# A third buffer for the second feed-forward weights, two small fp4 tiles fewer, and the planner's due times set anew

## The chip, the cores and the metric

The kernel runs on one core of one Trainium2 chip, as one program. The metric is the device time of one execution in microseconds; the time of a kernel is the median of several runs. TensorE (PE) does the matrix products and its share of the transposes, VectorE (DVE), ScalarE (ACT) and GpSimd (POOL) work on tiles in SBUF, and all transfers are issued by SyncE (SP), whose queue is in order.

## What is computed

The input has 8 sequences of 1024 rows with 256 columns. Four blocks follow each other, each added to its input after a plain layer norm of it:

```python
x = x + L0_attn(layernorm(x))   # linear "flow" attention, 16 heads of 16, cumulative sums along the
                                # sequence; Wo; layer norm; gelu(h @ W1 + b1) @ W2 + b2, 256 -> 1024 -> 256;
                                # layer norm
x = x + L0_ffn(layernorm(x))    # relu(x @ w1 + b1) @ w2 + b2, 256 -> 1024 -> 256
x = x + L1_attn(layernorm(x))   # softmax attention, one head of 256, over the whole sequence
x = x + L1_ffn(layernorm(x))    # fp4: silu(q(x) @ q(wg).T) * (q(x) @ q(wu).T), then q(h) @ q(wd).T, 256 -> 704 -> 256
# q: blocks of 16, scale = max|x| / 6, each element rounded to the fp4 grid and multiplied by the scale
```

All of it is in float32.

## The kernel before, in words

The rows are cut into 64 chunks of 128, and four chunks make a group: `flows` is 16 groups, two for each sequence. Each part of the work is a Python generator: `linear_group`, `linear_span` and `linear_chunk` for the linear attention, `dense` for both feed-forward networks of 1024, `norms_1` and `norms_2` behind each of these, `soft_chunk` for softmax attention and the fp4 network, `fp4_weights` and `softmax_weights` for their weights. A generator yields what it needs next: an engine, the tiles that must be done, how many PSUM banks, and a due time `at`, counted in groups.

**The planner.** `Plan.run` chooses which generator goes on. It keeps a model time for each engine (`Plan.took` holds the costs), takes the part that can start soonest on PE's model clock, and among parts that could start now the one with the smallest due time. The order in which instructions are issued is pinned on all five engines, so the choices are made when the program is built, and on the chip each engine follows its list. The due times come from the table `T`; `EARLY` holds other values for stretches of PE's model time (until 130, 260, 400 and 2150 us), and where a name isn't in the stretch's own table, `T` holds. `weights` is the due time of the weight loads, `prods`, `sums`, `weighted`, `scores`, `chunk`, `xo`, `turn_h`, `turn_k` of steps of the linear attention, `soft`, `soft1` and the like of the softmax chunks; names with a number at the end (`lin1`, `weights0`) are added for that group alone. `ripe_*` says how long before PE needs it a part of each engine counts as ripe.

**Turning tiles.** `flip` transposes a tile of 128x256 in one of two ways. By DMA: POOL splits the floats into halves of 16 bits (`cut`), SP issues a DMA transpose (`spun`), ACT joins them again. On PE: two matmuls with the identity, and one copy by ACT. It takes PE where `plan.idle(1, times["ahead"])` finds that no other part would be ready for PE within `ahead` microseconds of the model, and in the first group.

**Filling.** Where the planner sees PE wait for more than 1.6 us, `fill` issues matmuls of the identity up to a little before the time at which the next part is expected.

**Weights of the dense networks.** They are not kept in SBUF: `load_weights` inside `dense` loads them again for each group, 256 KB at a time, two blocks `f` in one tile. `w_in` is the first matrix of each network, `w_out` the second; each has two buffers, and one tile serves both halves of a group through repeated loads. The rule for a load is

```python
at=p + 0.9 + due("weights", p) + (2 * n % 32 + (0 if first else LAG)) / 32,
when=lambda: n < bufs + used[0] // 2 and count["stage"] >= 2,
unused=ws[n - bufs :][:1] if n >= bufs else (),
```

with `bufs` from `W_IN` or `W_OUT`: load `n` may be issued when the tile `bufs` loads before it has been used up. `half` is a turned half of a group's activations, the moving operand of the products with `w_in`; `hidden` is the result after gelu or relu, and `second` multiplies it with `w_out`.

**fp4.** `fp4` quantizes a tile in place: `x_amax` (block maxima), `x_s` (scales), `x_r` (their reciprocals), then four passes of DVE and one of ACT. The scale tiles are small tiles in rotation, `x_s` of four buffers and `x_r` of three.

All engines' instructions carry line 417 in the profile, the line that issues them in `Queue`; so groups are told apart by the tiles' names.

Of the kernel before, what the change touches and what calls it, by code (L numbers as in the profile page):

```python
# [17 lines left out]
P = 128  # L18
# [5 lines left out]
INTER = 704  # L24
V_PADS = 2
HB = P // 2
SCW = P + HB
W_IN, W_OUT = 2, 2
RES = 10
HALVES = 5  # L30
T = dict(
    span=-0.073, prods=0.129, pair=0.137, sums=0.037, weighted=0.239, sums2=0.231, chunk=0.625,
    scores=0.819, turn_k=0.829, xo=0.419, turn_h=0.635, step=0.092, dense=-0.115, norm=0.522,
    soft=3.5, soft1=0.277, soft2=0.575, soft3=0.75, fp4=2.397, fp4_over=4.836, tail=11,
    weights=0.209, shy=0.745, ripe_t=1.247, ripe_v=0.744, ripe_s=0.298, ripe_g=0.0, ripe_d=6.94,
    back=0.511, ahead=0.946, stage=3, lin=0.0, lin0=0.01, lin1=0.0, lin2=0.0, lin3=0.0,
    dense0=0.0, dense1=-0.033, norm0=0.0, norm1=0.0, weights0=-0.412, weights1=0.023, gate0=0,
    gate1=1, by_act=1,
)
LAG = 2  # L40
QB = 16
# [35 lines left out]

EARLY = [
    (130.0, dict(
        prods=0.359, pair=0.052, weighted=0.011, sums2=0.405, scores=0.861, turn_k=0.81,  # L80
        xo=0.296, step=0.131, dense=0.051, soft=2.551, soft1=0.323, soft2=0.706, fp4_over=5.754,
        weights=0.044, ripe_t=1.058, ripe_v=0.456, ripe_s=0.249, ripe_g=0.541, ripe_d=9.276,
        lin3=0.344, dense1=-0.003, weights0=-1.017, weights1=0.043,
    )),
    (260.0, dict(
        span=-0.064, prods=0.185, sums=-0.114, chunk=0.702, scores=0.785, dense=-0.085,
        soft=3.213, soft1=0.121, weights=-0.008, ripe_s=0.838, back=0.505, lin=-0.259,
        lin0=-0.325, norm0=-0.157, norm1=-0.26, weights0=-0.379, weights1=0.063, gate1=3.5,
    )),
    (400.0, dict(  # L90
        prods=-0.044, turn_k=0.82, turn_h=0.707, step=0.103, norm=0.746, soft=3.784, soft3=0.912,
        fp4=2.195, weights=0.078, ripe_d=7.2, ahead=0.839, lin2=-0.414,
    )),
    (2150.0, dict(
        chunk=0.596, xo=0.47, norm0=-0.113, pair=0.211, sums=0.071, turn_h=0.706, dense0=-0.017,
        ripe_d=6.945, ahead=0.541, weighted=0.176, lin3=-0.528, soft3=1.013, prods=0.106,
        gate1=3, fp4=3.733, lin1=0.497, dense1=0.151, turn_k=0.801, weights=0.169, lin2=-0.186,
    )),
]

# [18 lines left out]
class Plan:  # L119
# [206 lines left out]
    def dve(self, *tiles, **kw):  # L326
        return self.need("vector", tiles, **kw)

    def act(self, *tiles, **kw):
        return self.need("scalar", tiles, **kw)  # L330
# [39 lines left out]
    def run(self):  # L370
        while self.parts:
            now = self.free.get("tensor", 0.0)
            best = None
            for part in self.parts:
                t = self.ready(part[1])
                if t is None:
                    continue
                stays = self.tiled and part[1].tiled
                queue = part[1].queue
                wait = max(max(t) - now - (0.3 if stays or part[2] < 0.0 else 0.0), 0.0)  # L380
                urgent = part[2] < 0.0
                unripe = 0.0 if urgent else max(t[1] + self.times[RIPE[queue]] - now, 0.0)
                key = wait, unripe, queue == "tensor", not stays, part[2]
                if best is None or key < best[0]:
                    best = key, part, max(t)
            assert best is not None, "every part waits for another"
            until = max(now, best[2])
            if until - self.ran > 1.6 and best[1][1].queue == "tensor" and self.fill is not None:
                if (self.banks_free(best[1][1].banks + 1) or 0.0) <= self.ran + 0.4:
                    self.fill(until - 0.6)  # L390
                    self.ran = until - 0.6
            if best[0][0] > 0.0 or best[1][1].queue == "tensor":
                self.free["tensor"] = max(now, best[2])
            part = best[1]
            need = next(part[0], None)
            if need is None:
                self.parts.remove(part)
            else:
                part[1] = need
                if need.at is not None:  # L400
                    part[2] = need.at
# [34 lines left out]
def block_stack_kernel(ctx: ExitStack, tc: tile.TileContext, a: dict, out: bass.AP):  # L436
# [50 lines left out]
    def fresh(kind, need, name=None):  # L487

        need.fresh = kind
        yield need  # L490
        return make(kind, name)
# [16 lines left out]
    def small(shape, name, bufs=4):  # L508
        t = sm.tile(shape, F32, tag=name, name=name, bufs=bufs)
        return t  # L510
# [275 lines left out]
    def blocks(t, width):  # L786
        return t[:, :width].rearrange("p (b e) -> p b e", e=QB)

    def wide(v, rows, nb):
        return v.unsqueeze(2).to_broadcast([rows, nb, QB])  # L790

    def fp4(src, width, rows=P, factor=1.0):

        nb = width // QB
        src = src[:rows, :width]
        amax = small([P, INTER // QB], "x_amax", 2)[:rows, :nb]
        nc.vector.tensor_reduce(
            amax, blocks(src, width), AX.X, ALU.max, apply_absolute_value=True
        )
        sc = small([P, INTER // QB], "x_s", 4)[:rows, :nb]
        nc.vector.tensor_scalar(sc, amax, factor / 6.0, 1e-12, ALU.mult, ALU.max)
        rc = small([P, INTER // QB], "x_r", 3)[:rows, :nb]
        nc.vector.reciprocal(rc, sc)  # L810
        yield dve(rc)
        nc.vector.scalar_tensor_tensor(
            blocks(src, width),
            blocks(src, width),
            -factor * (1.0 - 2.0**-23),
            wide(rc, rows, nb),
            ALU.mult,
            ALU.mult,
        )
        tile_c = yield from fresh("q_c", act(src))  # L820
        c = tile_c[:rows, :width]
        nc.scalar.activation(c, src, AF.Square, scale=(2.0**22 / 6.0) ** 0.5)
        yield dve(c)
        k = 2.0**22 * 4.0 / 3.0
        nc.vector.scalar_tensor_tensor(src, c, k, src, ALU.add, ALU.add)
        yield dve(src)
        nc.vector.scalar_tensor_tensor(src, c, k, src, ALU.add, ALU.subtract)
        plan.drop(tile_c)
        nc.vector.tensor_tensor(
            blocks(src, width), blocks(src, width), wide(sc, rows, nb), ALU.mult  # L830
        )

    def fp4_weights():
# [15 lines left out]
        for i, (src, turns) in enumerate(pieces):  # L849
            for j in range(i, min(i + 3, len(pieces))):  # L850
                if j not in raws:
                    ahead = pieces[j][0]
                    raws[j] = (yield from fresh(
                        "soft",
                        dma(at=times["fp4"] + times["fp4_over"] * i / len(pieces), when=lambda: count["stage"] >= times["stage"]),
                        "w_raw",
                    ))[
                        : ahead.shape[0], : ahead.shape[1]
                    ]
                    nc.sync.dma_start(out=raws[j], in_=ahead)  # L860
            rows, width = src.shape
            raw = raws.pop(i)
            at = times["fp4"] + times["fp4_over"] * i / len(pieces)
            yield dve(raw, at=at)
            yield from fp4(raw, width, rows)
            yield pe(raw, banks=1)
            bank = tr_bank()
            for k, (dst, c0, n) in enumerate(turns):
                nc.tensor.transpose(bank[:n, k, :rows], raw[:, c0 : c0 + n], ident[:rows, :rows])
            plan.drop(raw)  # L870
            yield act(bank)
            for k, (dst, c0, n) in enumerate(turns):
                nc.scalar.copy(dst, bank[:n, k, :rows])
# [55 lines left out]
    weights = set()  # L929
# [753 lines left out]
    def soft_chunk(cc):  # L1683
# [81 lines left out]
        n = yield from layernorm("soft", rows)  # L1765
        yield dve(n)
        yield from fp4(n, D)
        xqT = two((yield from fresh("soft", plan.pool(n, at=at + times["soft2"]), "xqT")))
        yield from flip(two(n), xqT, last=n)
# [26 lines left out]
        plan.drop(xqT)  # L1796
        yield dve(hid)
        yield from fp4(hid, INTER, factor=0.5)
        hqT, pairs = [], []
        for half in range(2):  # L1800
# [92 lines left out]
```

## Time and profile before

| | |
|---|---|
| median of three runs | 2453.99 us (2453.81 to 2455.13) |
| the profiled execution | 2454.87 us, span 2453.2 us |
| PE busy | 2423.9 us, 99% of the span, 16475 matmuls |
| DVE, ACT, POOL busy | 1915.0, 1390.8, 1276.8 us |
| mean granted clock of PE | 0.997 |
| w_out and w_in loads | 256 each, of 256 KB |
| DMA transposes | 770 |

The profile is of one execution. Times are in microseconds unless marked ns. PE is the matmuls, PEld the loads of the stationary operand beside them, SPq SyncE's queue. A row of a group reads: line, engine, operation, output<-inputs by tile names, shape, count; then busy time and mean of one in ns; then the idle time of the engine just before them and what ended it. A row of a stretch reads: its limits, its length, then for each engine the busy time and the number of instructions, then PE's granted clock, the busy share of the DMA engines and GB/s. A row of the order of time reads: start, duration, engine, line, operation, with the idle time before it and what ended that in brackets. `bank<-ident` with no other input is a filler; `bank<-ident,x` turns tile x on PE.

### The profile page before, as it was taken

How to read it: one execution, taken by the hardware profiler on the slowest of the kernel's cores; microseconds unless marked ns; L12 is line 12 of the kernel's file. 1: busy time of each engine (PE TensorE's matmuls, PEld its weight loads, DVE VectorE, ACT ScalarE, POOL GpSimd, SP SyncE). 2: the span in 40 equal slices, each digit the busy share in tenths (PEclk: the TensorE clock that was granted, in tenths of full speed). 3: DMA queues.
4: the chain of work that ended last, by engine and by line, in shares of the span. 5: the costliest groups of instructions: out<-in, count | busy, mean ns of one | idle time of the engine just before them, and what ended most of it. 6: DMA issues, size and time to landing. Idle time of an engine off the chain costs nothing.

```text
span 2453.2 us, 47660 instructions
## 1 busy us (share of the span) xinstructions
PE 2423.9 (99%) x16475; PEld 1893.4 (77%) x16475; DVE 1915.0 (78%) x4149; ACT 1390.8 (57%) x2901; POOL 1276.8 (52%) x2260
## 2 busy tenths in 40 slices
PE   8999999999999999999999999999999999999998
PEld 6878777777777777777777777787777777877766
DVE  7778787878779787787877887688786977755877
ACT  5454556565565645556565565655556565555563
POOL 4354556565555656365563655546455574544342
PEclk9999999999999999999999999999999999999999
DMA  3255455564655555546555555555555555545342
GB/s 106 82 158 159 123 153 127 138 145 121 145 136 123 136 140 129 139 114 155 132 121 134 127 151 127 132 133 129 139 129 130 138 124 140 126 130 124 71 85 54
DMA packets 631985, 313.00 MB, mean 128 GB/s; under 512 B 435392, under 2 KB 620224, under 8 KB 631744
## 3 DMA queue, kind: packets, MB, share of 16 engines
q1 hardware_dynamic: 631744, 309.96, 51.1%
q8 instruction: 130, 2.13, 0.4%
q14 instruction: 111, 0.91, 0.1%
HBM read 188.17 MB, written 20.71 MB: 85 GB/s over the span
## 4 chain that ended last, share of the span: by engine, by line
PE 85%; DVE 8%; POOL 2%; DMA 2%; issue 1%; ACT 1%; SPq 0%; DVEq 0%; POOLq 0%; ACTq 0%
PE bank L417 85%; DMA spun<-cut 2%; DVE hid L417 1%; DVE prod L417 1%; POOL cut L417 1%; DVE n L417 1%; DVE ln_st L417 1%; POOL ln_rstd L417 1%; DVE x_amax L417 0%; DVE sc L417 0%; DVE mx L417 0%; DVE q L417 0%; DVE u L417 0%; DVE k L417 0%; POOL ln_shift L417 0%
## 5 line engine op out<-in xcount | busy, mean ns | idle before, releaser
L417 PE MATMUL bank<-half,w_in 128*128 128x256 f32 x2048 | 530.1, 382 | 8.5 <-ACT half L417 7.2
L417 PE MATMUL bank<-w_out,hidden 128*128 128x256 f32 x2048 | 526.2, 384 | 0.9 <-DMA w_out<-in_L_attn_W_dram 0.8
L417 PEld LDWEIGHTS bank<-w_out,hidden 128*128 128x128 f32 x2048 | 378.1, 190 | 103.6 <-issue 45.7
L417 PEld LDWEIGHTS bank<-half,w_in 128*128 128x128 f32 x2048 | 385.2, 190 | 87.8 <-issue 22.7
L417 POOL TENSOR_SCALAR ln_ve<-ln_mv 128x1 f32<-128x1 f32 x384 | 107.4, 280 | 544.0 <-DVE ln_mv L417 525.0
L417 POOL TENSOR_TENSOR ln_rstd<-ln_ve,neghalf 128x1 f32<-128x1 f32 x384 | 250.4, 652 | 32.0
L417 ACT ACTIVATE hidden<-bank,c_L_ffn_b 128x256 f32<-128x256 f32 x256 | 120.7, 472 | 226.6 <-PE bank L417 225.1
L417 PE MATMUL bank<-n2T,qT 128*128 128x512 f32 x512 | 241.4, 594 | 0.1
L417 PE MATMUL bank<-vt,probT 128*128 128x256 f32 x1024 | 231.6, 379 | 0.0
L417 PEld LDWEIGHTS bank<-vt,probT 128*128 128x128 f32 x1024 | 194.1, 190 | 32.1 <-issue 6.0
L417 POOL COPY cut<-n 128x512 uint16<-128x512 uint16 x233 | 175.6, 759 | 80.9 <-DVE n L417 67.4
L417 ACT ACTIVATE hidden<-bank,c_L_attn_b 128x256 f32<-128x256 f32 x256 | 119.7, 469 | 172.0 <-PE bank L417 171.2
L417 POOL COPY cut<-prob 128x512 uint16<-128x512 uint16 x215 | 147.6, 708 | 88.5 <-ACT prob L417 51.9
L417 POOL COPY cut<-hid 128x512 uint16<-128x512 uint16 x169 | 114.4, 694 | 148.6 <-DVE hid L417 51.1
L417 PE MATMUL bank<-wdT,hqT 128*128 128x256 f32 x768 | 176.2, 379 | 0.0
L417 PE MATMUL bank<-wgT,xqT 128*128 128x352 f32 x512 | 173.8, 462 | 1.2 <-ACT xqT L417 1.2
L417 PE MATMUL bank<-wuT,xqT 128*128 128x352 f32 x512 | 172.4, 459 | 0.0
L417 ACT COPY probT<-spun 128x512 uint16<-128x512 uint16 x254 | 162.0, 674 | 12.7 <-DMA spun<-cut 12.3
L417 ACT ACT_TABLE_LOAD x126 | 161.7, 1283 | 4.4 <-PE bank L417 2.1
L417 PEld LDWEIGHTS bank<-wdT,hqT 128*128 128x128 f32 x768 | 145.4, 190 | 23.0 <-issue 1.2
L417 PEld LDWEIGHTS bank<-n2T,qT 128*128 128x128 f32 x512 | 96.3, 190 | 70.5 <-issue 56.4
L417 PEld LDWEIGHTS bank<-wuT,xqT 128*128 128x128 f32 x512 | 97.3, 190 | 54.2
(272 smaller groups left out, 4838.2 us busy)
## 6 DMA issues: line engine op xcount, KB each, us to landing
w_in<-in_L_attn_W_dram SPq DMA_DIRECT2D x128, 256.0 KB
w_out<-in_L_attn_W_dram SPq DMA_DIRECT2D x128, 256.0 KB
w_in<-in_L_ffn_w_dram SPq DMA_DIRECT2D x128, 256.0 KB
w_out<-in_L_ffn_w_dram SPq DMA_DIRECT2D x128, 256.0 KB
spread<-packed SPq DMA_DIRECT2D x90, 256.0 KB
spun<-cut SPq DMA_TRANSPOSE x770
x<-in_L_attn_inputs_dram SPq DMA_DIRECT2D x64, 128.0 KB
xr<-in_L_attn_inputs_dram SPq DMA_DIRECT2D x64, 128.0 KB
```

The lines of the kernel that those rows point to most:

```text
L417: ins = method(*args, **kw)
```

## The change

`W_OUT` goes from 2 to 3: a third buffer for the second matrix, 2 KB more in each partition. `x_s` goes from four buffers to three and `x_r` from three to two. The tables of `EARLY` get other values in all stretches, and a fifth table holds from 2150 on, where `T` alone held before. `fill` stops 1.0 us before the expected time and no longer 0.6.

```diff
-W_IN, W_OUT = 2, 2
+W_IN, W_OUT = 2, 3
...
 EARLY = [
     (130.0, dict(
-        prods=0.359, pair=0.052, weighted=0.011, sums2=0.405, scores=0.861, turn_k=0.81,
-        xo=0.296, step=0.131, dense=0.051, soft=2.551, soft1=0.323, soft2=0.706, fp4_over=5.754,
-        weights=0.044, ripe_t=1.058, ripe_v=0.456, ripe_s=0.249, ripe_g=0.541, ripe_d=9.276,
-        lin3=0.344, dense1=-0.003, weights0=-1.017, weights1=0.043,
+        prods=0.359, pair=0.052, weighted=0.011, sums2=0.405, chunk=0.557, scores=0.861,
+        turn_k=0.81, xo=0.296, turn_h=0.656, step=0.131, dense=0.051, soft=2.551, soft1=0.323,
+        soft2=0.706, fp4_over=5.754, weights=0.08, ripe_t=1.058, ripe_v=0.456, ripe_s=0.249,
+        ripe_g=0.541, ripe_d=9.276, lin3=0.344, dense1=-0.003, weights0=-1.017, weights1=0.043,
     )),
     (260.0, dict(
-        span=-0.064, prods=0.185, sums=-0.114, chunk=0.702, scores=0.785, dense=-0.085,
-        soft=3.213, soft1=0.121, weights=-0.008, ripe_s=0.838, back=0.505, lin=-0.259,
-        lin0=-0.325, norm0=-0.157, norm1=-0.26, weights0=-0.379, weights1=0.063, gate1=3.5,
+        span=-0.064, prods=0.34, sums=-0.114, weighted=0.339, chunk=0.702, scores=0.945,
+        dense=-0.085, soft=3.213, soft1=0.121, weights=-0.008, ripe_s=0.794, back=0.505,
+        lin=-0.259, lin0=-0.325, lin2=-0.983, dense1=-0.028, norm0=-0.157, norm1=-0.26,
+        weights0=-0.379, weights1=0.063, gate1=3.5,
     )),
     (400.0, dict(
-        prods=-0.044, turn_k=0.82, turn_h=0.707, step=0.103, norm=0.746, soft=3.784, soft3=0.912,
-        fp4=2.195, weights=0.078, ripe_d=7.2, ahead=0.839, lin2=-0.414,
+        span=-0.031, prods=-0.044, sums=0.149, scores=0.9, turn_k=0.82, step=0.103, norm=0.746,
+        soft=3.876, soft2=0.578, soft3=0.912, fp4=2.195, fp4_over=4.172, weights=0.238,
+        ripe_d=7.2, ahead=0.839, lin=0.187, lin2=-0.414, turn_h=0.816,
     )),
     (2150.0, dict(
-        chunk=0.596, xo=0.47, norm0=-0.113, pair=0.211, sums=0.071, turn_h=0.706, dense0=-0.017,
-        ripe_d=6.945, ahead=0.541, weighted=0.176, lin3=-0.528, soft3=1.013, prods=0.106,
-        gate1=3, fp4=3.733, lin1=0.497, dense1=0.151, turn_k=0.801, weights=0.169, lin2=-0.186,
+        prods=0.036, pair=0.211, sums=0.071, weighted=0.176, chunk=0.596, turn_k=0.801, xo=0.47,
+        turn_h=0.596, soft3=1.013, fp4=3.733, fp4_over=6.383, weights=0.104, ripe_d=6.945,
+        ahead=1.487, lin1=0.497, lin2=-0.186, lin3=-0.528, dense0=-0.017, dense1=0.151,
+        norm0=-0.113, norm1=0.103, weights0=-0.286, gate1=3,
+    )),
+    (1000000000.0, dict(
+        lin3=0.54, ripe_d=5.647, lin1=0.423, dense1=-0.052, scores=0.51, xo=0.287, chunk=0.609,
+        shy=0.81, back=0.523, sums2=0.353, weights0=-0.388, soft1=0.394, step=0.139,
+        ripe_v=1.456, ripe_s=0.503, ahead=1.562, lin=-0.002,
     )),
 ]
...
                 if (self.banks_free(best[1][1].banks + 1) or 0.0) <= self.ran + 0.4:
-                    self.fill(until - 0.6)
-                    self.ran = until - 0.6
+                    self.fill(until - 1.0)
+                    self.ran = until - 1.0
...
-        sc = small([P, INTER // QB], "x_s", 4)[:rows, :nb]
+        sc = small([P, INTER // QB], "x_s", 3)[:rows, :nb]
...
-        rc = small([P, INTER // QB], "x_r", 3)[:rows, :nb]
+        rc = small([P, INTER // QB], "x_r", 2)[:rows, :nb]
```

## The prediction

> **What bounds the kernel now.** I read the page first: busy times (part 1), and the slices (part 2).
>
> ```profile
> span 2453.2 us, 47660 instructions
> PE 2423.9 (99%) x16475; PEld 1893.4 (77%) x16475; DVE 1915.0 (78%) x4149; ACT 1390.8 (57%) x2901; POOL 1276.8 (52%) x2260
> PE   8999999999999999999999999999999999999998
> ```
>
> TensorE (PE) bounds it: it stands still for 2453.2 - 2423.9 = 29.3 us. A better order of the same work can win only that, the filler matmuls of the identity that the planner puts into expected gaps (the second row below, from the groups by form: 36.6 us), and matmuls run at the lower clock. All else on PE is in both kernels. So I asked where these three lie. First PE in stretches of the plan:
>
> ```profile
> L417 PE MATMUL bank<-w_out,hidden 128*128 128x256 f32 x2048 | 526.2, 384 | 0.9 <-DMA w_out<-in_L_attn_W_dram 0.8
> L417 PE MATMUL bank<-ident 128*128 128x128 f32 x288 | 36.6, 286 | 3.1 <-POOL ident masks.py:199 3.1
> 0.00:130.00 130.00, 117.87 (x1053) 95.65 (x1054) 98.28 (x234) 62.98 (x164) 48.28 (x102) 0.96 0.34 99
> 130.00:260.00 130.00, 125.45 (x1098) 102.38 (x1097) 105.19 (x254) 67.00 (x162) 66.56 (x128) 0.99 0.54 149
> 994.00:1288.00 294.00, 293.24 (x1999) 229.07 (x1998) 234.40 (x498) 170.57 (x350) 162.88 (x283) 1.00 0.54 133
> 2400.00:2453.20 53.20, 45.79 (x224) 35.34 (x222) 40.03 (x72) 19.47 (x37) 12.09 (x15) 1.00 0.21 50
> ```
>
> The second column is PE's busy time. Idle: 12.1 us before 130, 4.6 us from there to 260, 7.4 us after 2400, 0.76 us in a period of 294 us (two groups) of the steady part. Filler: 29.2 us (226 of 288) before 400, the other 7.4 us after 2400. From 260 to 2400 little is to be had: the waits of PE say 4.7 us on `half` (the six seams where the next group's turned activations arrive), and 0.3 us else.
>
> The one wait on `w_out` stands in the order of time at 208 us, just behind one on `w_in`:
>
> ```profile
> 202.90 1.89 PE L417 MATMUL bank<-half,w_in 128*128 128x256 f32 x8
> 206.11 1.13 PE L417 MATMUL bank<-half,w_in 128*128 128x256 f32 x4 [1.31 <-DMA w_in<-in_L_attn_W_dram]
> 208.02 1.78 PE L417 MATMUL bank<-w_out,hidden 128*128 128x256 f32 x4 [0.78 <-DMA w_out<-in_L_attn_W_dram]
> 209.59 1.91 PE L417 MATMUL bank<-half,w_in 128*128 128x256 f32 x4
> 211.30 1.24 PE L417 MATMUL bank<-w_out,hidden 128*128 128x256 f32 x4
> 212.37 1.72 PE L417 MATMUL bank<-ident 128*128 128x128 f32 x14
> 214.15 1.13 PE L417 MATMUL bank<-half,w_in 128*128 128x256 f32 x4
> ```
>
> Both weights come late, matmuls then run slow, and a filler stands before the next. The windows around it show the clock (busy time, then the granted clock after the bracket):
>
> ```profile
> 204.89:208.30 3.41, 1.41 (x5) 1.00 0.98 299
> 208.30:211.71 3.41, 3.41 (x9) 0.50 1.05 270
> 243.90:247.30 3.40, 1.84 (x60) 1.00 0.96 166
> 247.30:250.70 3.40, 3.38 (x61) 1.00 0.21 43
> ```
>
> A stretch of 3.41 us with 1.41 us of work was followed by 3.41 us at 0.50; one with 1.84 us was not. The other two drops of this trace follow stretches with 1.53 us (13.74 to 17.15) and 1.00 us (30.80 to 34.22).
>
> **The change part by part.** All sums are on the profiled execution: 2454.87 us, its span 2453.2 plus 1.7 around it; the median of the runs is 2453.99, so I take 0.9 us off at the end.
>
> 1. *Third `w_out` buffer.* No byte and no instruction is added: the 256 loads stay, each issued up to one tile earlier. Its direct price now is all the idle time before 2048 matmuls: 0.9 us, 0.78 of it at 208. Its indirect worth is in SP's order: a `w_out` load waits in SP for PE to release a buffer, and transposes, spreads and `w_in` queue behind it. At 202.97 `w_in` was issued, at 205.22 four `spread` loads, and the DMA engines were at 0.98 of their time (299 GB/s) when PE starved. With `w_out` already there, `w_in` and `w_out` needn't both be fetched in that burst. The stall costs 1.31 + 0.78 idle, 1.55 of half clock (12 matmuls from 208.02 to 212.16 in 4.14 us, at 0.216 each 2.59), and 1.78 of filler until 214.15: 5.4 us. Gone wholly: -5.4; moved elsewhere: 0. `w_in` keeps two buffers and is the first of the two late, so I take -4.0.
>
> 2. *Small scale tiles, 4 to 3 and 3 to 2.* Written by DVE and read by DVE in order; the trace shows no idle time before any `x_s` or `x_r` instruction. Nothing, hidden by DVE's own order. If a third quantization had to wait for a tile, one final multiply (892 ns) would be moved forward: up to +0.9 at a place, on an engine that is 78% busy. 0.
>
> 3. *Fill up to 1.0 us instead of 0.6 before the expected time.* Thirteen blocks of filler, each some 0.4 us shorter (5.2 us in all). This wins only where the filler still ran when the awaited tile was there. By the order of time: n was ready at 13.63 and turned at 13.94; `n0T` at 17.04, used 17.98; h at 66.76, turned 67.14; h at 101.67, turned 103.13; k long before 59.39; `hqT` at 2444.24, used 2444.71. Six blocks at most 0.4 each: -2.3. Against it: a longer gap can cost a clock drop, 3.41 / 2 = 1.7 us. The only gap that now follows a mid-run block is 0.53 (at 109.84), so 0.93 after the change, well short of the emptiness of the stretches that dropped. I take -1.5, bounds -2.3 to +1.7.
>
> The Trainium skill has a rule that bears on this: "TensorE: Matmul & The Clock Gate", Part 1, "What's actually happening", puts the half clock after at least one idle window of about 3.4 us. Taken as a wholly idle window, no gap of this kernel would cost clock and the longer margin would be free (-2.3); the rows above disagree, since a window 41% busy was followed by 0.50.
>
> 4. *Due times before 260.* They move DVE's and SP's order. Two waits stand out: the filler from 101.34 to 109.31, about 8 us while DVE finishes two h between scans, and 241.62 to 247.32, 1.88 of filler and 1.52 idle before `half`. In the new numbers the first stretch has chunk and turn_h of its own, the second later prods, weighted and scores, so other DVE work stands behind the layer norms. Both gone: -11.4. But DVE was busy 76% there (98.28 of 130), the two h still need 2.3 us of normalizing each, and new gaps open for the closed ones: bounds -6 to +5; I take -2.5.
>
> 5. *Due times of 260 to 2150, with `ahead` 0.541 to 1.487.* Five seams at 0.76 and one at 0.93 are 4.7 us. `ahead` asks whether PE has other work within that time; a larger one turns fewer tiles on PE and more by POOL, SP and DMA. From 400 to 2150 PE turns 34 blocks of n, k and h, 0.108 us each: 3.7 us, of which at most all is won. A turn by DMA takes a cut (0.7 us on POOL), a transpose (1.2 us on SP) and a copy (0.67 instead of 0.37 on ACT), and half of that path is what the seam waits on. Bounds -6 (both) to +8 (1.0 us more at each of eight seams); I take -2.5, as PE's own work is what bounds this part.
>
> 6. *A last stretch after 2150.* To 2400 PE is busy 249.94 of 250, so nothing. After 2400 there are 7.4 us idle and 7.4 us of filler, but that part follows DVE's chain of fp4 steps (0.8 to 0.9 us each on the chain of waits), which the change doesn't shorten; larger `ahead` takes the short way away there. -4 to +4; I take -1.0.
>
> 7. *What the third buffer adds.* Earlier `w_out` loads stand before transposes in SP's queue: 0.42 us of issue each, 256 KB in the DMA engines. Seen once per group in 16 groups, a tenth of it at a seam that shows: +0.5; and for gaps that open at new places I add +2.0, about the size of the largest wait now (1.9).
>
> Sum: -4.0 - 1.5 - 2.5 - 2.5 - 1.0 + 0.5 + 2.0 = -9.0. 2454.87 - 9.0 = 2445.9 profiled, 2445.0 for the median.
>
> **The rivals.** *No difference* (2449 to 2459): PE is 99% busy, the idle time on w_out is 0.9 us, and for each gap closed one of like size opens. For it: the steady part, 1750 us long, has almost nothing to give; against: before 130 alone there are 12.1 us idle and eight blocks with 196 of the 288 fillers (about 25 us), which one new order in the right direction cuts. I would put it at 2452, the certain -1.5 of step 3 and 0.5 from step 1. That the third buffer isn't used at all, because a due time and not a free buffer starts each load, belongs here for step 1 and leaves the rest: 2449.
>
> *Slower*: the load that is pulled forward meets the seam. In each of 16 groups PE waits at the seam for `half`, that is for the last transposes in SP's queue. If one `w_out` load is issued before them, they start 0.42 us later and share the DMA engines with 256 KB: the `w_in` load of 202.97 took until 206.1, 3.1 us. Priced at 1.0 us a group: +16, less 6 us of the gains at the start: 2454 + 10 = 2464. It decides as soon as a seam of the steady part shows over 1.0 us where it now shows 0.76 in two groups; past about 1.9 us of idle in 3.41 each would cost 1.7 us of clock besides. For it: 70.6 us in which POOL's cuts wait for transposes; against: the due time still orders the load, and `half` waits for a transpose that was itself late because of its cut.
>
> **How the numbers follow.** Faster as worked out: 0.66, 2445.0; its own range, by the bounds of steps 1, 3, 4, 5, 6 of which not all fall one way, 2431 to 2449. No difference: 0.13. Slower: 0.21, of which about half above 2462. The range 2431 to 2463 leaves out some 0.08 below and 0.10 above. 0.2% of the time, 4.9 us, is about what a measurement of this kernel can tell from no change; the chances for more, within and less than that are those of the three cases.
>
> **What would show it.** Right: no wait of PE on `w_in` or `w_out` near 205 and no half clock after 41 us; PE idle before 260 below 14 us (now 16.7) and filler in all below 32 us; the period of the steady part still 293 to 294 us, a span near 2444. Step 1 is wrong if PE waits there on `w_in` alone; step 3 if the clock drops more than three times after the first; step 5 if the seam gaps add up to over 6 us or the period grows; step 6 if the idle time after 2400 grows. Wrong as a whole: PE idle plus filler at or above 66 us, or a period above 295 us.

## The result: slower by 0.19%, and the profile after

The changed kernel takes 2459.79 us (median, 2457.36 to 2461.92), the kernel before on the same chip 2454.71 us (2452.63 to 2457.15): a ratio of 1.0019, 95% interval 1.0013 to 1.0026. The forecast was 2445.0. The profiled execution was the quickest of the changed kernel's runs, 2457.36 us with a span of 2455.3; so the trace shows 2.1 us of the loss (2455.3 - 2453.2), and the rest lies in its other runs, of which no trace is at hand. The mean granted clock of the sixteen was 0.9968, 0.998 in this one.

The page of the changed kernel: busy times, then from the groups by form the second matrix' products, the filler, and the layer norm output turned on PE; then four windows as before (limits, length, busy time of PE, PEld, DVE, ACT and POOL, clock, DMA share, GB/s).

```profile
span 2455.3 us, 47506 instructions
PE 2422.2 (99%) x16449; PEld 1887.9 (77%) x16449; DVE 1903.0 (78%) x4148; ACT 1393.5 (57%) x2906; POOL 1247.7 (51%) x2245
L425 PE MATMUL bank<-w_out,hidden 128*128 128x256 f32 x2048 | 523.1, 384 | 1.0 <-ACT hidden L425 0.9
L425 PE MATMUL bank<-ident 128*128 128x128 f32 x232 | 29.7, 286 | 3.1 <-POOL ident masks.py:199 3.1
L425 PE MATMUL bank<-ident,n 128*128 128x128 f32 x66 | 13.3, 292 | 5.2 <-ACT n L425 3.2 <-DVE n L425 1.9
0.00:130.00 130.00, 116.46 (x1029) 93.61 (x1030) 98.98 (x236) 63.45 (x165) 47.44 (x103) 0.97 0.37 103
130.00:260.00 130.00, 124.73 (x1089) 101.83 (x1087) 104.16 (x247) 62.53 (x157) 59.75 (x114) 0.99 0.53 151
994.00:1288.00 294.00, 293.49 (x2001) 228.21 (x2000) 233.02 (x494) 166.97 (x349) 159.55 (x279) 1.00 0.55 132
2400.00:2455.30 55.30, 49.19 (x229) 38.26 (x227) 42.34 (x83) 22.57 (x42) 13.65 (x21) 1.00 0.29 62
```

PE is busy 1.7 us less than before and idle 33.1 us instead of 29.3. The filler fell by 6.9 us, as it should; but before 260 PE is idle 18.8 us, not 16.7, and it turns more tiles itself (`n` 66 times instead of 46). The waits on the load of `w_out` are gone. The stall at 208 isn't:

```profile
205.96 1.03 PE L425 MATMUL bank<-w_out,hidden 128*128 128x256 f32 x4
210.12 1.87 PE L425 MATMUL bank<-half,w_in 128*128 128x256 f32 x4 [3.13 <-DMA w_in<-in_L_attn_W_dram]
211.78 1.91 PE L425 MATMUL bank<-w_out,hidden 128*128 128x256 f32 x4
213.49 1.14 PE L425 MATMUL bank<-half,w_in 128*128 128x256 f32 x4
```

That is PE in order of time. PE now starves once, 3.13 us on `w_in` alone, where it starved 1.31 on `w_in` and 0.78 on `w_out`. SP's queue in order of time says why:

```profile
201.06 2.50 SPq L425 DMA_DIRECT2D spread<-packed  x4
203.61 0.60 SPq L425 DMA_DIRECT2D w_out<-in_L_attn_W_dram  x1
204.25 0.47 SPq L425 DMA_DIRECT2D w_raw<-in_L_ffn_w_down_dram  x1
204.82 1.70 SPq L425 DMA_DIRECT2D w_in<-in_L_attn_W_dram  x2
```

The two loads of `w_in` are issued at 204.82, behind four `spread` loads, a `w_out` load and one of fp4 weights. The DMA engines were full meanwhile (1.00 of their time from 206.9 to 210.3; that window is shown at the end). The tile of the first of the two was last read by PE at 203.53 (the end of the matmuls of the load two before it), 1.3 us before its issue. So with two tiles the turn in the queue can hold at most 1.3 of the 3.13 us. The load then took 5.3 us from its issue to its use, where the one issued at 202.97 in the kernel before took 3.1; how much of that is the full DMA engines was not tested alone.

*Where the time went.* To see where in the run it was won and lost, I took from both traces the time at which PE had done the same useful matmuls: each counted at its usual distance from the next, fillers and turns on PE left out. The difference, after minus before, at eight times of the kernel before:

```
time in before (us)    121    248    295    406   1163   2336   2387    end
after                 -0.9   -6.8   +1.3   +1.0   -0.3   +6.7   +6.1   +1.9
```

So the start did win 6.8 us by 248. It lost 8.1 in the next 47 us (2.9 of gaps, 1.8 of filler, 1.1 of turns on PE, 2.3 of small delays), held until 1163, lost 7.0 in the second half of the steady part, and won 4.2 at the end. The total of +1.9 is made of -6.3 filler, -1.7 half clock, +3.2 turns on PE, +3.6 gaps, and +3.0 of delays between matmuls too small to be listed as idle time. A turn or a filler counts here at its usual distance, some 0.11 us; if the delay behind each turn is counted to the turn, the turns are +5.4 and the small delays +1.0.

The loss behind 248, PE in order of time in the changed kernel:

```profile
265.89 1.13 PE L425 MATMUL bank<-w_out,hidden 128*128 128x256 f32 x4
266.86 1.95 PE L425 MATMUL bank<-ident 128*128 128x128 f32 x16
...
274.58 0.41 PE L425 MATMUL bank<-ident,w_raw 128*128 128x128 f32 x2 [1.47 <-DVE w_raw L425]
274.99 2.86 PE L425 MATMUL bank<-half,w_in 128*128 128x256 f32 x12
...
279.14 1.13 PE L425 MATMUL bank<-w_out,hidden 128*128 128x256 f32 x4 [0.86 <-ACT hidden L425]
```

and in the kernel before:

```profile
272.37 1.99 PE L417 MATMUL bank<-w_out,hidden 128*128 128x256 f32 x8
274.20 1.03 PE L417 MATMUL bank<-wo,xo 128*128 128x256 f32 x4
275.28 1.89 PE L417 MATMUL bank<-half,w_in 128*128 128x256 f32 x8
```

The dense products of the first groups come to their end earlier (267.0 instead of 274.4), but the next group's first product with `w_in` starts at 274.99 against 275.28. Before, dense products reached to within 0.9 us of it. Now filler, turns and a wait stand between: as I read it, the work pulled forward had been the stock that bridged this place. The next group's linear attention began later on PE (its first `sc,v_pad` product at 255.0, before at 249.5), and DVE, which feeds it, was busy 32.89 us of 248 to 296, before 39.09.

*The steady part.* The distance from the first `w_in` product of a group to that two groups later, for groups 4 to 13:

```
before  296.9 291.8 294.1 294.1 294.1 294.1 294.1 294.1 294.1 290.6
after   299.7 293.4 298.7 299.8 290.5 286.5 290.7 301.5 302.2 288.1
```

Before, the schedule falls into a cycle of 294.1 us; after, it never does. This isn't the seam. From 400 to 2400 the waits of PE are in the kernel before

```profile
PE bank L417 <- ACT half L417: 4.7, 6, 0.9
PE bank L417 <- DVE hid L417: 0.3, 1, 0.3
```

and in the changed one (total, times, longest; the four largest):

```profile
PE bank L425 <- ACT half L425: 1.9, 2, 1.5
PE bank L425 <- DVE n L425: 1.5, 1, 1.5
PE bank L425 <- DVE sc L425: 1.2, 1, 1.2
PE bank L425 <- ACT xqT L425: 0.5, 1, 0.5
```

The seam fell from 4.7 to 1.9 us, and five other waits came. The idle sum is nearly the same there (5.9 after, 5.2 before). The 7.0 us lost from 1163 to 2336 are 1.6 of gaps, 0.7 of turns and 4.6 of small delays; PE switches 126 times instead of 108 between products on 32 rows or columns and products on the whole array in that stretch. That this costs it is not shown: `tuned_2buf` below, the fastest order, switches 130 times there.

### The profile page after: what moved, and what is told of

Its sections match the earlier page's. It is cut to its first block, busy times and chain, and to the rows that moved or that the text cites. A ratio compares the mean times of both kernels' runs of the same rounds, so it can differ in the third digit from the quotient of the medians.

```text
span 2455.3 us, 47506 instructions
## 1 busy us (share of the span) xinstructions
PE 2422.2 (99%) x16449; PEld 1887.9 (77%) x16449; DVE 1903.0 (78%) x4148; ACT 1393.5 (57%) x2906; POOL 1247.7 (51%) x2245
## 4 chain that ended last, share of the span: by engine, by line
PE 91%; DVE 5%; DMA 1%; ACT 1%; POOL 1%; issue 1%; SPq 0%; DVEq 0%; POOLq 0%; ACTq 0%
PE bank L425 91%; DVE prod L425 1%; DMA spun<-cut 1%; DVE hid L425 1%; DVE n L425 0%; DVE u L425 0%; DVE spread L425 0%; DVE x_amax L425 0%; DVE ln_st L425 0%; POOL ln_rstd L425 0%; DVE div L425 0%; DMA w_in<-in_L_attn_W_dram 0%; ACT L425 0%; DVE e L425 0%; DVE x_r L425 0%
## 5 line engine op out<-in xcount | busy, mean ns | idle before, releaser
L425 POOL TENSOR_SCALAR ln_ve<-ln_mv 128x1 f32<-128x1 f32 x384 | 101.8, 265 | 584.5 <-DVE ln_mv L425 543.6
L425 POOL TENSOR_TENSOR ln_rstd<-ln_ve,neghalf 128x1 f32<-128x1 f32 x384 | 236.2, 615 | 32.0
L425 PEld LDWEIGHTS bank<-vt,probT 128*128 128x128 f32 x1024 | 193.9, 190 | 29.3 <-issue 2.6
L425 POOL COPY cut<-prob 128x512 uint16<-128x512 uint16 x225 | 167.9, 770 | 86.4 <-ACT prob L425 45.5
L425 POOL COPY cut<-n 128x512 uint16<-128x512 uint16 x223 | 158.4, 716 | 83.5 <-DVE n L425 52.9
```

Of the source, the lines that this page charges most:

```text
L425: ins = method(*args, **kw)
```

## The experiments

All ratios are to the kernel before, which ran beside each kernel in five rounds on the same chip; its median on the four chips used was 2454.85 to 2455.31 us.

### Is a third tile worth anything by itself?

First the order of before, with three tiles behind `w_out`; the planner still counts two, so that no instruction moves, and a load's wait is one tile further back. Also the same for `w_in`.

```diff
# old_order_3buf                       # old_order_3in: bufs=3 if first else 2
# (both also x_s 4 to 3 and x_r 3 to 2)
-w = big.tile([P, 2, 2 * P], F32, tag=tag, name=tag, bufs=bufs)
+w = big.tile([P, 2, 2 * P], F32, tag=tag, name=tag, bufs=2 if first else 3)
```

Expected of the third `w_out` tile in the old order:

> The kernel before with three w_out tiles in SBUF while the planner still counts two (small scale tiles 3 and 2): every engine's list is that of before, only SP waits less for PE before a w_out load. This is the worth of the third buffer by itself. If a w_out load that waits for PE holds up SP's queue, as my prediction said: 2450 to 2453, the weights stall at 206 shortened. Theory O (only the order counts, and the planner already places a load where its buffer is free): within 1.5 us of before, ratio 0.9995 to 1.0005.

Expected of the third `w_in` tile in the old order:

> The kernel before with three w_in tiles (two for w_out), the planner counting two: the list of before on every engine. If w_in's tile is what is short: the 1.31 us at 206 goes, and the 0.78 on w_out behind it too, with the half clock 3 to 5 us less: 2450 to 2452. If its place in the queue is: 2454 to 2456, the wait stays over 1 us.

Measured: 2454.06 us with the `w_out` tile, 0.9996 (0.9988 to 1.0005), and 2453.95 us with the `w_in` tile, 0.9995 (0.9986 to 1.0003). Neither can be told from no change. PE in order of time with the third `w_out` tile:

```profile
207.17 1.13 PE L417 MATMUL bank<-half,w_in 128*128 128x256 f32 x4 [1.24 <-DMA w_in<-in_L_attn_W_dram]
208.87 1.83 PE L417 MATMUL bank<-w_out,hidden 128*128 128x256 f32 x4 [0.56 <-ACT hidden L417]
```

The wait on `w_out` is gone, as the change says; the one on `w_in` just ahead of it stays, and 0.56 of a wait on `hidden` takes the freed place. With the third `w_in` tile PE still waited on `w_in` there, first PE and then SP's queue in order of time:

```profile
205.21 1.13 PE L417 MATMUL bank<-half,w_in 128*128 128x256 f32 x4 [1.00 <-DMA w_in<-in_L_attn_W_dram]
213.00 1.13 PE L417 MATMUL bank<-half,w_in 128*128 128x256 f32 x4 [2.12 <-DMA w_in<-in_L_attn_W_dram]
204.51 2.51 SPq L417 DMA_DIRECT2D spread<-packed  x4
207.06 1.10 SPq L417 DMA_DIRECT2D w_in<-in_L_attn_W_dram  x2
```

The load for the second wait was issued at 207.06, right behind the `spread` loads and with a tile free: as long as the order is kept it comes late because it is issued late. What a planner that counts three `w_in` tiles would do wasn't tried.

Then the planner is told of the third tile, under the due times of before; and the changed kernel goes back to two.

```diff
# old_wout3 (also x_s 4 to 3 and x_r 3 to 2)
-W_IN, W_OUT = 2, 2
+W_IN, W_OUT = 2, 3
# new_wout2: the opposite line in the changed kernel, tables and margin kept
```

Expected of the planner's third buffer under the old due times:

> The kernel before with the third w_out buffer alone (and the small scale tiles 3 and 2, which alone change no instruction and no wait); due times and margin of before. My prediction's steps 1 and 7: -3.5 (-5.4 to +0.5), the waits on weights at 206 to 208 gone: 2451. Theory B: +3 to +6, with a longer wait on w_in: 2458 to 2461. Theory O: the buffer by itself is worth nothing sure, 2451 to 2458 by the other order that it brings.

Expected of the changed kernel with two buffers:

> The changed kernel with two buffers for w_out again; due times, margin and small tiles stay as changed. Theory B: the third buffer lets w_out loads stand before w_in in the SP queue, so the 3.1 us wait on w_in at 210 is its price; without it that wait falls below 1.5 us and the time is 2453 to 2456. Theory O: the wait on w_in near 210 stays over 2 us, and the time is 2456 to 2464, since the due times were set with three buffers. Theory M: 2459.

Measured: 2482.68 us, 1.0112 (1.0099 to 1.0126), and 2472.45 us, 1.0075 (1.0062 to 1.0088). The third buffer alone, with no other number touched, costs 28 us, and taking it out of the changed kernel costs 12.7. PE's waits on `w_out` have no part in the first; its groups are

```profile
L417 PE MATMUL bank<-w_out,hidden 128*128 128x256 f32 x2048 | 523.4, 383 | 0.1
L417 PE MATMUL bank<-ident 128*128 128x128 f32 x396 | 49.9, 285 | 3.1 <-POOL ident masks.py:199 3.1
```

No wait on `w_out`, and 13 us more filler than before. The other choice of loads has changed the order of everything. In the terms of the table above its lag is +8.6 at 121, +19.2 at 406, +24.6 at 1163 and +28.2 at the end. The order of before with a third tile in SBUF costs nothing: so the 28 us come from the order, not from the tile.

The two small scale tiles, three and two of them, were in `old_order_3buf` and `old_order_3in` as well: the order is that of before on every engine, and neither there nor in the changed kernel does an engine sit idle before an `x_s` or `x_r` instruction. They have no run by themselves.

### The margin of the filler

```diff
# old_margin10 in the kernel before; new_margin06 the opposite in the changed one
-self.fill(until - 0.6)
-self.ran = until - 0.6
+self.fill(until - 1.0)
+self.ran = until - 1.0
```

Expected of the longer margin in the kernel before:

> The kernel before with the fill margin at 1.0 us alone; the order on every engine is that of before, only fillers are fewer. My prediction's step 3: -1.5 (-2.3 to +1.7), 2453. Theory M: the clock drops more often, +3 to +5, 2458 to 2460, lower mean clocks. Theories O and B: within 2 us of before.

Expected of the shorter margin in the changed kernel:

> The changed kernel with the fill margin back at 0.6 us; the order on every engine stays that of the changed kernel, only fillers are added (about 4 for each of 12 blocks). Theory O (order): the new due times cost the 5 us, between 1163 and 2336 us above all; the margin matters little: 2458 to 2460, ratio to before 1.0015 to 1.0025. Theory M (margin): the longer gaps (2.9 us at 31, 3.1 at 210 in the profile) drop the clock in more executions than before; with 0.6 the time falls to 2455 to 2456 (ratio 1.000 to 1.0007) and the mean clocks rise by 0.001. Theory B (buffer): like O here, 2459.

Measured: 2453.15 us, 0.9993 (0.9985 to 1.0002), and 2461.07 us, 1.0024 (1.0015 to 1.0033). Only the fillers' number differs in each pair. In the kernel before it is

```profile
L417 PE MATMUL bank<-ident 128*128 128x128 f32 x246 | 31.4, 285 | 3.1 <-POOL ident masks.py:199 3.1
```

42 fillers fewer, 5.2 us of PE's busy time, and 1.7 us of time (2454.85 - 2453.15); in the changed kernel 1.3 (2461.07 - 2459.79). Neither is clear of the noise (the first interval reaches 1.0002, and that of the second overlaps the changed kernel's 1.0013 to 1.0026); both have the size that step 3 gave.

### The tables, one at a time

```diff
# old_tail_table: before, margin 1.0, and the new last table
+    (1000000000.0, dict(lin3=0.54, ripe_d=5.647, lin1=0.423, ...)),
# old_newmid: before, margin 1.0, and the new table of 400 to 2150
# new_old_mid: the changed kernel with the old table of 400 to 2150
# new_old_400: the changed kernel with the old table of 260 to 400
# new_scores785: the changed kernel, one due time of 130 to 260 put back
-        ... scores=0.945,
+        ... scores=0.785,
```

Expected of the new last table in the old order:

> The kernel before with the margin of 1.0 us and the new last table from 2150 on, nothing else new: the order up to 2150 is that of before. The margin alone gave 0.9993. In the changed kernel's profile the stretch behind 2387 us took about 4 us less than before. If that comes from the table, 2449 (ratio 0.9978); if it only gave back what the stretch before had lost, 2453 or more (0.999 to 1.001).

Expected of the old middle table in the changed kernel:

> The changed kernel with the table for 400 to 2150 of before; all else as changed, the same order up to 400. In the profile the changed kernel loses 7 us on before between 1163 and 2336. If the new middle table is the cause (my step 5 said -2.5 for it), the old one gives 2452 to 2455 here. If due times fit only the state that they were set in, it is slower than the changed kernel: 2463 to 2475.

Expected of the old table of 260 to 400 in the changed kernel:

> The changed kernel with the table for 260 to 400 of before; the same order up to 260. In the profile the changed kernel is 6.8 us ahead of before at 248 and 1.3 behind at 296. If the new third table costs that, the old one gives 2452 to 2455; if tables fit only the state that they were set in, 2463 or more.

Expected of the new middle table in the old order:

> The kernel before with the new table for 400 to 2150 and the margin of 1.0 us; two buffers, the same order as before up to 400. If the new middle table is better by itself and only suffers from the changed start (my step 5: -2.5): 2450 to 2453. If it fits only the state that it was set in: 2460 to 2470, and no repeating cycle of 294.1 us for two groups.

Expected of the one due time put back:

> The changed kernel with one due time of before: scores=0.785 instead of 0.945 in the table for 130 to 260. In the changed kernel the second sequence's first group attends at 255.0 us against 249.5, and PE runs dry between 266.6 (end of group 1's dense work) and 275.0 (first product of group 2). If that due time alone holds the attend step back, it is won: 2452 to 2455. If due times fit only together (the order is one whole): slower than the changed kernel, 2465 or more.

```
                  us        ratio (95% interval)        lag in the trace at 295, 1163, 2336, end
old_tail_table    2453.70   0.9995 (0.9986 to 1.0004)   -2.3   -1.6   +0.7   -2.4
old_newmid        2469.77   1.0059 (1.0045 to 1.0073)   -2.5   +5.0  +10.8  +11.9
new_old_mid       2461.72   1.0026 (1.0016 to 1.0036)   +1.0   +0.4   +8.0   +5.5
new_old_400       2476.67   1.0088 (1.0075 to 1.0102)   +2.9  +10.7  +23.7  +19.0
new_scores785     2491.45   1.0148 (1.0134 to 1.0162)   +8.0  +19.8  +37.6  +36.9
```

The last table by itself adds nothing to the margin it was tried with (0.9995 against 0.9993): its trace loses 2.3 us from 1163 to 2336 and wins 3.1 behind. The middle table alone isn't what loses the steady part: with the old one put back the changed kernel still loses 7.6 us from 1163 to 2336 (7.0 without). But on the old order the new middle table costs some 16 us (1.0059 against 0.9993). No table that was tried has a worth of its own: every single part, put into or taken out of either set, made the kernel slower or changed nothing. One due time, `scores` of a stretch that ends at 260, costs 32 us, and of its lag at the end 29 come after 295, in stretches whose numbers are those of the changed kernel.

### Setting further, with two buffers and with three

If due times must be set as a whole, the fair question on the third buffer is what each gives after more setting of the same kind. I moved due times on from both kernels by the planner's own model time and ran what came out.

```diff
# tuned_2buf: before, margin 1.0, 11 due times moved or set in four tables, and a last table of six
 130: +sums=0.1, +back=0.532    260: scores .785 -> .888, +lin3=0.083, +ripe_d=7.241
 400: +norm0=-0.061, +ripe_t=1.787, +dense1=0.04
2150: sums .071 -> .221, dense0 -.017 -> -.092, +shy=0.632
last: norm=0.56, back=0.355, fp4=2.579, soft=4.701, soft2=0.444, soft1=0.373
# tuned_3buf: the changed kernel, 13 due times moved
 260: dense1 -.028 -> -.307, +ripe_t=0.942    400: span -.031 -> -.214, soft3 .912 -> 1.11, +ripe_s=0.178
2150: soft3 1.013 -> .927, ripe_d 6.945 -> 5.896, +lin=0.035, +step=0.108
last: ripe_d 5.647 -> 3.35, +norm=0.446, +soft2=0.738, +soft3=0.925
# tuned_3buf_b: the changed kernel, 19 others moved (ripe_t, ripe_d, turn_h, lin2, lin3, soft, ...)
# tuned2_out3, tuned2_in3: tuned_2buf's order, a third tile behind w_out or behind w_in
# (both also x_s 4 to 3 and x_r 3 to 2)
```

Expected of the two-buffer version:

> The kernel before (two w_out buffers) with the margin of 1.0 us and some 20 due times moved, a last table from 2150 on among them, found in the same way and with as many steps as the three-buffer one. If the gain lies in the due times and not in the buffer: 2443 to 2447 or better. If the third buffer is needed for it: 2450 or more.

Expected of the three-buffer version:

> The changed kernel (three w_out buffers, margin 1.0) with 13 due times moved further: in the table to 260 dense1=-0.307, ripe_t=0.942; to 400 span=-0.214, soft3=1.11, ripe_s=0.178; to 2150 soft3=0.927, ripe_d=5.896, lin=0.035, step=0.108; in the last ripe_d=3.35, norm=0.446, soft2=0.738, soft3=0.925. If the third buffer and the due times can win what my prediction counted on (idle and filler at the start and the end, seams), 2433 to 2440 (ratio 0.991 to 0.994), with less idle, filler and fewer changes of PE between small and whole tiles. If the order's cost is chance, 2450 to 2470.

Expected of the other three-buffer version:

> The changed kernel (three w_out buffers, margin 1.0) with another set of 19 due times moved, found like those of the two-buffer kernel (2448.95). If three buffers cost nothing with fitting due times: 2449 to 2453 and a steady part near 294.1 us for two groups. If the early w_out loads keep w_in late, the wait on w_in near 210 is over 3 us again and the time 2455 to 2465.

Expected of the two-buffer order with a third `w_out` tile:

> The two-buffer kernel with moved due times (2448.95 us), with three w_out tiles in SBUF, the planner still counting two: the same list on every engine. PE waits there 1.08 us on w_out and 3.5 us on w_in (205 to 222 us). If w_out is the short buffer: 1.1 us and the half clock behind it, 1.5 to 3 us less, 2446 to 2447.5. If w_in is: within 1 us of 2449, the w_in waits unchanged.

Expected of the two-buffer order with a third `w_in` tile:

> The same kernel with three w_in tiles instead, the planner counting two: the same list on every engine. If w_in is the short buffer: its waits of 1.18, 1.76 and 0.56 us go, 2444 to 2447. If what w_in waits for is its place in SP's queue behind the four spread loads, not a free tile: the waits stay over 2 us in all, within 1 us of 2449.

```
                us        ratio (95% interval)        lag in the trace at 295, 1163, 2336, end
tuned_2buf      2448.95   0.9975 (0.9965 to 0.9985)   +0.4   -2.6   +0.1   -5.9
tuned_3buf      2459.10   1.0016 (1.0008 to 1.0025)   +5.5   +3.7   +7.0   +4.6
tuned_3buf_b    2463.08   1.0033 (1.0021 to 1.0044)   +7.5   +5.8  +11.9   +8.3
tuned2_out3     2447.49   0.9972 (0.9962 to 0.9982)
tuned2_in3      2448.43   0.9970 (0.9958 to 0.9981)
```

The two-buffer version beats both kernels, the one before by 0.25%. Against before, all that it wins lies behind 2336 (+0.1 there, -5.9 at the end), where its own last table holds. A third tile under that order changes nothing that can be told from it, for either matrix; PE's wait on `w_out` near 208 stays at 1.0 us with a third `w_out` tile, and its two on `w_in` at 1.9 and 1.3 with a third `w_in` tile. The version's page, and PE's waits on weights between 200 and 230 in it (line 396 is the issuing line, since the tables are written shorter):

```profile
span 2447.2 us, 47580 instructions
PE 2422.2 (99%) x16449; PEld 1888.0 (77%) x16449; DVE 1905.4 (78%) x4130; ACT 1400.9 (57%) x2920; POOL 1245.2 (51%) x2253
PE bank L396 <- DMA w_in<-in_L_attn_W_dram: 2.9, 2, 1.8
PE bank L396 <- DMA w_out<-in_L_attn_W_dram: 1.1, 1, 1.1
PE bank L396 <- DMA w_in<-in_L_ffn_w_dram: 0.6, 1, 0.6
```

PE is busy exactly as long as in the changed kernel, 2422.2 us, in a span 8.1 us shorter. And at 200 to 230 it waits 4.6 us for weights, more than either kernel. The stall that the prediction counted on isn't where the difference between these two is. Most of it is in the steady part (from +0.9 us at 295 to +6.6 at 2336, by the two rows of lags): the distance of two groups is 292.5, 294.2 and then 294.1 to 294.3 but for the last (288.3). The two three-buffer versions stay above the changed kernel's own lag at 295; `tuned_3buf` has distances near 294 again (293.4 to 295.9 but for the first and the last), yet keeps what it lost at the start. PE's wait on `w_in` near 210 is 5.56 us in `tuned_3buf` and 2.90 in `tuned_3buf_b`: no order found with three buffers is rid of it. One search with two buffers and two with three don't show that three can't do as well.

## Why the prediction was wrong

**The sum.** -9.0 was forecast for the profiled execution and +2.5 measured (2457.36 - 2454.87). The mechanism of the chosen case, a better order of the same work, didn't take place over the whole run. The time lies inside the stated range, but the change went the other way. The opening, that all else on PE is in both kernels, left out the turns on PE and the delays between matmuls.

**Step 1, -4.0: wrong.** By itself the tile gave a ratio of 0.9996, -1.0 us with an interval from -2.9 to +1.2, and in the changed kernel the stall still costs 3.13 idle and 1.7 of half clock where 5.4 were to go. (The 1.55 of half clock in that sum sets twelve matmuls against 4.14 us, which hold eleven distances; it is 1.7 to 1.8.) The prediction had the right rows: `w_in` was the first of the two late, and the DMA engines were full. The four `spread` loads stood behind that load in the kernel before (205.22 against 202.97), and ahead of it only in the changed one; PE had last read its tile at 200.26, so no tile was short there either. It had also named the test ("wrong if PE waits there on `w_in` alone"), and that is what the trace shows, 3.13 us. The failing step is the indirect worth, the choice between the ends, 0 and -5.4: with the second wait taken away, the first stayed (1.24 of 1.31) and PE waited 0.56 for `hidden` in place of 0.78 for `w_out`.

**Step 2, 0: right as far as the traces show:** no order moves, and no engine sits idle before these tiles.

**Step 3, -1.5: right in size, as far as the runs can tell,** -1.7 and -1.3. The clock cost that it weighed didn't show as more drops: two in the trace of after, three before (none counted at the very end). The gap that it put at 0.93 is 1.42, before 108.92; with the old margin (`new_margin06`) it is 0.53. The longer one of 2.94 before 31.23 isn't the margin's: it is 2.96 there.

**Step 4, -2.5: the sign was right up to 248, wrong at 295.** With step 1 and 3 the start was to win 8; it won 6.8 at 248, 6.5 of it filler. The prediction set "new gaps" at +2.0 for the whole run. In the trace the gain was used up at the next group's start within 47 us. It hadn't asked when the next group would be ready: its `w_in` products didn't start earlier, so the work done earlier could only leave PE without work later.

**Step 5, -2.5: wrong, +7.0 from 1163 to 2336.** The seam did shrink, by 2.8 us, as counted. But the step took PE's gaps for separate items to be closed. In the kernel before, five of the six seams come once in each cycle of 294.1, with one other wait (0.3 us) from 400 to 2400; without the cycle five others came, 3.9 us in all, with more turns and, behind 1163, more small delays. The period was to stay at 293 to 294 and varies from 286.5 to 302.2; that was named as the sign of being wrong as a whole. Larger `ahead` was to lower the turns on PE; they went up, from 109 matmuls to 139. That came with the order and not with `ahead`: the changed kernel with the old middle table (`ahead` 0.541) has 137, and the order of before with the new one (1.487) has 105. That the middle table alone isn't the cause is shown (`new_old_mid`); that the state in which the schedule leaves the start matters is made likely by `new_old_400` and `new_scores785`, which change due times of the start only and lose most of their time after 400. What in that state decides whether the cycle sets in stays open. `old_wout3` reaches 294.1 late, from group 11, and is slowest but one: the cycle isn't enough. The changed order with only two tiles behind `w_out` wasn't tried.

**Step 6, -1.0: right in the changed kernel's trace (-4.2 after 2387, idle after 2400 from 7.4 to 6.1 us), but not as a term to be added:** on the old order the same table gives nothing.

**Step 7, +2.5: too small.** New gaps, turns and small delays came to +9.8 (3.6 + 3.2 + 3.0).

**The rivals.** "Slower" had the sign, but its mechanism didn't come: the waits on `half` at the seams fell to two, of which one (1.52 us at 496) is over 1.0. "No difference" had the nearer mechanism, one gap opened for each closed, and put it at 2452. The chance for faster, 0.66, rested on counting 12.1 us of idle time and 29.2 of filler before 400 as something that a new order "in the right direction" would cut, with nothing in the profile that told the direction.

## What to carry to other kernels

Where a hand-made order holds PE at 99%, the due times are one setting and not a list of gains: judge a new buffer or a new number only with the order held fixed (more tiles behind unchanged waits), and then with everything set again. Before a buffer is added for a late load, look at what stands ahead of that load in its queue: here a third tile took away the second of two late loads, and no gain could be told. And work done earlier on the busiest engine was no gain here, where what came next didn't start earlier.

## What the runs showed of the hardware

The granted clock goes by windows of 3.41 us on a fixed grid; all drops in a trace lie whole multiples of it apart. In the traces of all the kernels above, of the windows at full clock that ended between 6 us and 2440 us, those with at most 1.49 us of matmuls (44%) were followed by half clock 29 times of 29; those with 1.53 to 1.91 us 10 times of 35; those from 1.92 to 2.5 us never, 105 windows. Three such windows, each with the one that follows it (busy time and count of PE, clock, DMA share, GB/s): two of the changed kernel, and one of `tuned_3buf_b`:

```profile
206.90:210.30 3.40, 0.27 (x2) 1.00 1.00 294
210.30:213.70 3.40, 3.40 (x9) 0.50 0.04 10
...
493.60:497.00 3.40, 1.88 (x9) 1.00 0.58 114
497.00:500.40 3.40, 3.40 (x60) 1.00 0.36 95
```

```profile
1637.42:1640.83 3.41, 1.91 (x8) 1.00 0.50 135
1640.83:1644.24 3.41, 3.41 (x7) 0.50 0.23 63
```

So gaps need not be whole windows to cost 1.7 us (half of 3.41), and whether a gap of 1.5 to 2 us does can depend on where it falls on the grid: split between two windows it empties neither. What decides from 1.53 to 1.91 us stays open. The Trainium skill, "TensorE: Matmul & The Clock Gate", Part 1, "What's actually happening", states that the window runs freely, is 3413 ns long and doesn't restart with the kernel, which these traces agree with: drops lie 3.41 us or whole multiples apart, and the grid's first line falls 0.1 us behind the first instruction in the kernel before (17.15 less five windows) and 2.1 in the changed one (32.81 less nine). It puts the half clock after at least one idle window; here a window at most 44% busy was enough each time.
